# Two images side by side in a four-layer vision network: from "front and trunk" lanes to two whole-image lanes

## The chip, the cores and the metric

The kernel runs on one core of one Trainium2 chip. A core has five engines that run their own instruction queues in order: TensorE (PE, matrix multiply into PSUM), VectorE (DVE), ScalarE (ACT), GpSimd (POOL) and SyncE (SP, here used only to issue DMAs). The metric is the device time of one execution in microseconds; lower is better. All arithmetic is in float32.

## What is computed

The input is a batch of 4 images of 32x32 pixels and 384 channels. Every image passes four residual layers, each of the form `x = x + layer(group_norm(x))`. The images never meet: all reductions are within one image. Cut to what matters (one image, helper functions left out):

```python
# layer 0: deformable attention, 6 heads of 64 channels, 1024 queries and keys
q = gn(x) @ w_q + b_q
o = gelu(layernorm(grouped_conv3x3(q)))            # 6 groups
pos = tanh(o @ w_offp) * 16 + pixel_grid           # one sampling point per pixel and head
xs = bilinear_sample(gn(x), pos)                   # gathered pixels
k, v = xs @ w_k + b_k, xs @ w_v + b_v
bias = bilinear_sample(rpe, (grid - pos) * 0.5)    # [heads, 1024, 1024]
x = x + softmax(q k^T * scale + bias) v @ w_out + b_out

# layer 1: 12 heads of 32 channels, weighted by a group similarity
q, k, v = split(gn(x) @ Wqkv);  xg = gn(x) @ Wg + bg
gc = depthwise_conv3x3_stride2(xg)                 # 256 group centres
sim = sigmoid(beta + alpha * cos(xg, gc))          # [12, 1024, 256]
attn = softmax(q k^T) * (sim sim^T * gamma + 1 - gamma)
attn = attn / attn.sum(axis=query)                 # normalized over the queries
x = x + (attn v) @ Wproj

# layer 2: box sums over 5 columns and 20 channels, a quotient
# layer 3: outlook attention: 3x3 values weighted by softmax(gn(x) @ Wa), folded back
```

## The kernel before

The kernel is written against a tile framework: the Python code names tiles in pools and issues instructions, and the framework's scheduler puts the instructions of each engine in one order, places tiles in the buffers of their pools and writes the semaphores. The order in which the Python code issues work is the scheduler's priority; each engine then runs its own list strictly in that list's order.

The work on an image is cut in two parts, each written as a Python generator that yields after every small piece of work, with a number of "steps" that weighs the piece.

- **The front** (`Front.layer0`, 714 steps an image) is layer 0. `inputs0` (234 steps) loads the image, norms it, makes queries, runs the grouped convolution, computes the sampling points (`positions`), gathers pixels with indirect DMAs from the POOL queue (`gather`, line 652) and makes keys and values. Then come 12 calls of `head0` (6 heads, 2 halves of the queries, 38 steps each; with the divisions in `over_sums` 462 steps). For each of 8 blocks of 128 keys `head0` gathers a window of the bias table by an indirect DMA of POOL (line 734, tile `win`, 4 buffers), interpolates it in ACT (lines 746, 751) and DVE (747, 752), multiplies queries and keys on PE (755, into a PSUM tile `bank`), adds the two on DVE (756) and keeps a running maximum (761). Then it turns the maximum round over PE, POOL and ACT (768 to 780), and for each block subtracts it (787, DVE), takes the exponential (788, ACT) and multiplies with the values and with ones (790, PE, accumulated in one `bank` held through the 8 blocks). The output projection (18 steps) adds the residual and stores the image to DRAM.
- **The trunk** (`Trunk.image`, 1109 steps an image) is layers 1 to 3. `inputs1` (173 steps) norms, projects, runs the strided convolution and prepares softmax sums. Then come 6 calls of `pair` (two heads each, 118 steps): for each of 8 key blocks, PE makes logits (1154, into two PSUM tiles `big`), ACT exponentiates (1162), PE makes the group weights of both heads and both query halves (1184, four `bank` tiles, with transposes of kept blocks in line 1179), ACT copies parts that will be needed again (1192), DVE multiplies the weights into the exponentials (1193), and PE accumulates the values in the `bank` tile `av`, held through all 8 blocks (1128). Within the same step `sums_step` prepares the softmax sums of the next pair (1035 on PE, 1043 on DVE, 1044 on ACT, two `big` tiles). `layers23` is the tail: output projection (18 steps), layer 2 (93) and layer 3 (117).

PSUM has 8 banks: the pool `ps2` holds two tiles `big` of two banks each, the pool `ps1` four tiles `bank`. All work shares them. A pool `wts` holds three weight matrices, loaded by SP.

The main loop joins the two parts. `layer0(0)` runs the front of image 0 to its end. Then `layer3(b)` runs the trunk of image b step by step, and after each step advances the fronts of the following images until they are ahead by the trunk's share plus `LEAD` = 0.1. So trunk 0 runs with front 1, trunk 1 with front 2, trunk 2 with front 3, and trunk 3 alone. `Front` takes its tiles from the right side of SBUF, `Trunk` from the left. Front and trunk hand the image over through DRAM (`x1`).

Of the kernel before, what the change touches and what calls it, by code (L numbers as in the profile page):

```python
# [26 lines left out]
P = 128  # L27
# [24 lines left out]

R_LNG, R_LNB, R_BV0, R_BV3 = 0, C, 2 * C, 3 * C
R_BA = 4 * C
R_WOFFP = R_BA + 81
# [4 lines left out]


TRUNK_STEPS, FRONT_STEPS, LEAD = 1109.0, 714.0, 0.1

# [9 lines left out]
class Net:  # L73


    def __init__(self, ctx, tc, a):
        self.tc, self.nc, self.a = tc, tc.nc, a
        nc = self.nc
        pool = lambda name, bufs, **kw: ctx.enter_context(
            tc.tile_pool(name=name, bufs=bufs, **kw)  # L80
        )
        self.const = pool("const", 1)
        self.wts = pool("wts", 3)
        self.ps2 = pool("ps2", 2, space=PSUM)
        self.ps1 = pool("ps1", 4, space=PSUM)
        self.dram = pool("dram", 1, space=DRAM)
        self.n = 0
        self.consts()
        self.scratch()
        self.front, self.trunk = Front(self, "right"), Trunk(self, "left")  # L90

# [14 lines left out]
    def consts(self):  # L106
# [19 lines left out]
        self.rows = self.ct([P, NROW], "rows")  # L126
        nc.sync.dma_start(self.rows, a["rows"].partition_broadcast(P))
        self.blk = self.ct([P, P], "blk")
# [65 lines left out]
    def scratch(self):  # L194

        self.pairs = []
        for i in range(2):
            t = self.dram.tile([G * SLOTS, 2 * GC], F32, tag=f"pairs{i}", name=f"pairs{i}")
            self.pairs.append(t)
        dram = lambda name, shape: self.dram.tile(shape, F32, tag=name, name=name)  # L200

        self.x0 = [dram(f"x0_{i}", [C, N]) for i in range(2)]
        self.x1 = [dram(f"x1_{i}", [C, N]) for i in range(2)]

        self.qd, self.kd, self.xgd, self.yd = (dram(n, [C, N]) for n in ("qd", "kd", "xgd", "yd"))

        self.k0 = dram("k0", [C, N])
        self.gcd = dram("gcd", [C, M1])
        self.vd = dram("vd", [N, C])

        self.den = [dram(f"den{h}", [1, N]) for h in range(G)]
        self.rden = [dram(f"rden{h}", [1, N]) for h in range(G)]
        self.lse = [dram(f"lse{p}", [2, N]) for p in range(NH1 // 2)]
        self.skew = [
            self.dram.tile([NJ, P * ROWP], F32, tag=f"skew{i}", name=f"skew{i}")
            for i in range(2)
        ]
# [39 lines left out]
    def layer0(self, b):  # L257

        if b == 0:
            for _ in self.front.layer0(b):  # L260
                pass
            self.done = self.ahead = 0.0
            self.fronts = (w for i in range(1, NB) for w in self.front.layer0(i))

# [6 lines left out]
    def layer3(self, b, out):  # L271

        for w in self.trunk.image(b, out):
            self.done += w / TRUNK_STEPS
            while self.ahead < self.done + LEAD:
                self.ahead += next(self.fronts, FRONT_STEPS) / FRONT_STEPS
        assert self.ahead >= min(b + 1, NB - 1)


class Lane:  # L280


    def __init__(self, net, side):
        self.net, self.side = net, side

    def __getattr__(self, name):
# [112 lines left out]
class Front(Lane):  # L399
# [118 lines left out]
    def inputs0(self, b):  # L518
# [57 lines left out]
        for k in range(KC):  # L576
# [18 lines left out]
            yield 15  # L595
        oall = self.wt([P, NJ, C], "a12", 2)
        mv = self.wt([P, NJ, 2], "ln_mv")
        for j in range(NJ // 2):
# [24 lines left out]
        for j in range(NJ):  # L623
            v.tensor_scalar(
                oall[:, j, :],
                oall[:, j, :],
                mv[:, j, 0:1],
                rstd[:, j : j + 1],
                ALU.subtract,
                ALU.mult,  # L630
            )
            v.tensor_tensor(
                oall[:, j, :], oall[:, j, :], self.rows[:, R_LNG : R_LNG + C], ALU.mult
            )
            v.tensor_tensor(
                oall[:, j, :], oall[:, j, :], self.rows[:, R_LNB : R_LNB + C], ALU.add
            )
# [187 lines left out]
class Trunk(Lane):  # L825


    def image(self, b, out):
        with self.scope("l1y"):


            self.q4, self.k4 = self.wt([P, N], "q4"), self.wt([P, N], "k4")
            self.xg = self.wt([P, N], "xg")
# [14 lines left out]
    def inputs1(self, b):  # L848
        nc, v = self.nc, self.nc.vector
        x = self.wt([P, KC, N], "x")  # L850
        for k in range(KC):
            nc.sync.dma_start(x[:, k, :], self.x1[b % 2][k * P : (k + 1) * P, :])
        xh = self.wt([P, KC, N], "xh")
        self.norm(x, xh)
# [120 lines left out]
    def pair_tiles(self):  # L975
# [4 lines left out]
        nc = self.nc  # L980
        self.qks = [[self.wt([P, N], f"{t}{i}") for t in ("qa", "ka")] for i in range(2)]
        self.gc = self.wt([P, M1], "gc")
        for r in range(2):
            rest = slice(64 * r + HD1, 64 * r + 64)
# [6 lines left out]
    def load_sums(self, p):  # L991
# [3 lines left out]
        for h in range(2):  # L995
            rows = slice(64 * h, 64 * (h + 1))
            self.nc.sync.dma_start(self.q4[rows, :], self.qd[ch, :])
            self.nc.sync.dma_start(self.k4[rows, 0:512], self.kd[ch, h * 512 : (h + 1) * 512])

# [26 lines left out]
    def sums_step(self, i, st):  # L1026
# [4 lines left out]
        for h in range(2):  # L1031
            for r in range(2):
# [4 lines left out]
                    self.q4[rows, i * P : (i + 1) * P],  # L1037
                    self.k4[rows, 0:512],
                    start=True,
# [50 lines left out]
    def pair(self, p):  # L1090
# [6 lines left out]
        if p == 5:  # L1097

            for k, t in enumerate((self.q4, self.k4, self.xg[0:64, :])):
                nc.sync.dma_start(t, self.yd[k * P : k * P + t.shape[0], :])  # L1100
        vn = self.wt([P, NJ, 2 * HD1], "vp", 2)
        nc.sync.dma_start(
# [107 lines left out]
        values(*late.pop())  # L1210
        y = self.wt([P, 512], "y")
        nc.scalar.copy(y, av)
# [11 lines left out]
    def out1(self, b):  # L1224
# [3 lines left out]
        w = self.weights("Wproj")  # L1228
        y = (self.q4, self.k4, self.xg)
        self.mv = [self.moments() for _ in range(2)]  # L1230
# [25 lines left out]
    def layer2(self):  # L1256
        nc, v = self.nc, self.nc.vector
        with self.scope("l2"):
# [50 lines left out]

            dns = []  # L1310
            for ko in range(KC):
                ps = box20(den, ko)

                none = self.wt([P, N], "none", 2)
                v.tensor_scalar(none, ps, 0.0, None, ALU.is_equal)
                dn = self.wt([P, N], "dn", KC)
                v.scalar_tensor_tensor(dn, ps, 5.0, none, ALU.mult, ALU.add)
                x = self.x[:, ko, :]
                nc.gpsimd.tensor_tensor(x, none, x, ALU.add)
                dns.append(dn)  # L1320
            for ko in range(KC):
# [3 lines left out]
                v.tensor_tensor(x, dn, x, ALU.add)  # L1325
                self.stats(self.mv[1], self.x, ko)
                yield 14


    def layer3(self, b, out):  # L1330
        nc, v = self.nc, self.nc.vector
        skew = self.skew[b % 2]
        with self.scope("l3"):
# [97 lines left out]
            values(range(NJ // 2, NJ))  # L1431
            ys = []
            for i in range(NJ):
                pt = self.big()
                for k in range(KC):
                    nc.tensor.transpose(
                        pt[:, k * P : (k + 1) * P], self.x[:, k, i * P : (i + 1) * P], self.ident
                    )
                y = self.wt([P, C], "y", NJ)
                nc.scalar.copy(y, pt[:, 0:C])  # L1440
                ys.append(y)
            yield 20
            for i in range(NJ):
# [12 lines left out]
                v.tensor_tensor(y, ps[:, 0:C], y, ALU.add)  # L1456
                nc.sync.dma_start(out[i * P : (i + 1) * P, :], y)
                yield 4


# [82 lines left out]
```

## Time and profile before

| | us |
|---|---|
| median of 3 runs | 4879.74 |
| lowest and highest of them | 4869.65, 4883.42 |
| the profiled execution | 4916.4 |
| its span, first to last instruction | 4914.6 |
| PE busy in the span | 4251.9 (87%) |
| DVE busy | 3177.4 (65%) |
| ACT busy | 2331.1 (47%) |
| POOL busy | 934.4 (19%) |
| mean granted clock of PE | 0.905 |

The profiled execution is 0.75% longer than the median of the runs. "Busy" is the time in which an engine has an instruction under way; the granted clock is the share of its full clock that PE was given, and matmuls take longer where it is low. The times at which lines first and last appear in the trace cut the span into stages: the front of image 0 alone until about 643 us (line 432 ends it), trunk 0 with front 1 until about 1860, trunk 1 with front 2 until 3021, trunk 2 with front 3 until 4132 (line 1457 ends each), and trunk 3 alone to the end.

### The profile page before, as it was taken

To read this page: it belongs to the slowest core of one execution; us is meant where nothing else is said; L and a number is where in the kernel's file an instruction comes from. 1 tells how busy PE (TensorE), PEld (TensorE's weight loads), DVE (VectorE), ACT (ScalarE), POOL (GpSimd) and SP (SyncE) were. 2 spreads that over 40 slices of the span, in tenths; PEclk is the share of its full clock that TensorE was granted. 3 is DMA by queue.
4 is the path that set the end of the run, shared out by engine and by line. 5 is a ranking of instruction groups with operands and counts; after the bars stand their busy time and mean duration, and the time that the engine had idled before them with its cause. 6 is when DMAs were issued, how large, how long until landed. Compare 5 with 4: busy or idle time off the path is not lost.

```text
span 4914.6 us, 46753 instructions
## 1 busy us (share of the span) xinstructions
PE 4251.9 (87%) x15800; PEld 1829.4 (37%) x15800; DVE 3177.4 (65%) x5715; ACT 2331.1 (47%) x3623; POOL 934.4 (19%) x946
## 2 busy tenths in 40 slices
PE   5466677999999989889999989899999998999998
PEld 2222243333333453333333444343333335343444
DVE  3478827676878736577877763767687873455544
ACT  2155523565766213376666412356576721466630
POOL 1533203211212101331221110422121200000000
PEclk7677787999999989799999989799999998899998
DMA  5322244211212143331221123422121213201011
GB/s 116 106 81 87 69 128 143 92 55 38 76 47 74 33 145 111 104 95 49 66 58 58 55 75 111 151 88 58 32 78 44 78 34 111 91 24 30 18 38 39
DMA packets 230929, 366.84 MB, mean 75 GB/s; under 512 B 117476, under 2 KB 164673, under 8 KB 230689
## 3 DMA queue, kind: packets, MB, share of 16 engines
q1 hardware_dynamic: 169672, 197.36, 13.5%
q0 software_dynamic: 39936, 145.53, 9.7%
q10 hardware_dynamic: 21080, 20.96, 1.7%
q8 instruction: 125, 2.05, 0.2%
q14 instruction: 116, 0.94, 0.1%
HBM read 285.84 MB, written 78.21 MB: 74 GB/s over the span
## 4 chain that ended last, share of the span: by engine, by line
PE 50%; DVE 11%; ACT 11%; issue 5%; DMA 2%; POOL 1%; another core or an unknown queue 0%; SPq 0%; ACTq 0%; DVEq 0%; POOLq 0%
PE bank L1184 10%; PE big L376 5%; PE big L1154 5%; PE big L1035 4%; PE bank L755 4%; PE bank L790 4%; PE bank L390 3%; PE bank L1128 3%; ACT big L1044 3%; PE bank L1179 2%; PE big L1284 2%; DVE e L1193 2%; DVE nmax L1043 2%; ACT e L1162 1%; PE big L584 1%
## 5 line engine op out<-in xcount | busy, mean ns | idle before, releaser
L1193 DVE SCALAR_TENSOR_TENSOR e<-bank,gam,e 128x512 f32<-128x512 f32 x768 | 558.2, 749 | 568.3 <-ACT gn L1192 274.5
L1184 PE MATMUL bank<-sim,sg 128*128 128x512 f32 (+3 forms) x2304 | 879.6, 516 | 6.2 <-POOL sg L1139 3.7
L1044 ACT ACTIVATE big<-big,nmax 128x1024 f32<-128x1024 f32 x384 | 418.5, 1090 | 392.2 <-DVE nmax L1043 340.4
L734 POOL DMA_INDIRECT win<-strips,widx x384 | 421.2, 1097 | 876.6 <-DVE z L747 450.7
L1184 PEld LDWEIGHTS bank<-sim,sg 128*128 128x128 f32 x2304 | 408.7, 200 | 386.2 <-issue 303.6
L1162 ACT ACTIVATE e<-big 128x1024 f32<-128x1024 f32 x384 | 376.7, 1019 | 359.9 <-PE big L1154 354.7
L1043 DVE TENSOR_REDUCE nmax<-big 128x1 f32<-128x1024 f32 x384 | 453.7, 1219 | 74.4 <-PE big L1035 46.5
L1035 PE MATMUL big<-k,q 32*128 32x512 f32 x1536 | 353.6, 691 | 86.6 <-ACT e L1162 36.6
L1154 PE MATMUL big<-qa,ka 64*128 64x512 f32 x1536 | 412.9, 629 | 14.8 <-ACT big L1044 8.9
L1139 POOL TENSOR_SCALAR sg<-sim,gam 128x512 f32<-128x512 f32 x192 | 148.2, 774 | 1429.3 <-PE bank L1184 1135.5
L790 PE MATMUL bank<-lg,va 128*64 128x512 f32 x768 | 373.6, 635 | 39.8 <-ACT lg L788 39.7
L755 PE MATMUL bank<-qpad,kz 128*128 128x512 f32 x768 | 378.2, 622 | 21.4 <-DVE e L1193 13.2
L790 PE MATMUL bank<-lg,ones 128*64 128x512 f32 x768 | 372.9, 635 | 0.0
L746 ACT ACTIVATE z<-win,bias_f 128x528 f32<-128x528 f32 x384 | 277.2, 738 | 181.5 <-DVE lg L752 105.3
L752 DVE SCALAR_TENSOR_TENSOR lg<-z,bias_f,lg 128x512 f32<-128x512 f32 x384 | 300.8, 798 | 45.5 <-ACT lg L751 43.7
L747 DVE SCALAR_TENSOR_TENSOR z<-win,bias_f,z 128x528 f32<-128x528 f32 x384 | 292.0, 781 | 36.0 <-DMA win<-strips,widx 24.3
L652 POOL DMA_INDIRECT gat<-pairs,sidx x192 | 206.2, 1074 | 485.6 <-DVE ix_gt L464 241.6
L756 DVE TENSOR_TENSOR lg<-bank,lg 128x512 f32<-128x512 f32 x384 | 256.9, 685 | 60.3 <-PE bank L755 58.7
L787 DVE TENSOR_TENSOR lg<-lg,tb 128x512 f32<-128x512 f32 x384 | 250.6, 711 | 61.3 <-ACT tb L780 61.3
L751 ACT ACTIVATE lg<-z,bias_f 128x512 f32<-128x512 f32 x384 | 268.0, 719 | 44.3 <-DVE z L747 27.4
L788 ACT ACTIVATE lg<-lg 128x512 f32<-128x512 f32 x384 | 223.2, 630 | 85.4 <-DVE lg L787 85.1
L1154 PEld LDWEIGHTS big<-qa,ka 64*128 64x128 f32 x1536 | 135.8, 189 | 272.2 <-issue 157.0
(253 smaller groups left out, 5844.8 us busy)
## 6 DMA issues: line engine op xcount, KB each, us to landing
pairs<-xn SPq DMA_DIRECT2D x64, 192.0 KB
q<-qd SPq DMA_DIRECT2D x48, 256.0 KB
w<-in_gmat SPq DMA_DIRECT2D x16, 576.0 KB
w<-in_w_off SPq DMA_DIRECT2D x12, 576.0 KB
w<-in_Wqkv SPq DMA_DIRECT2D x12, 576.0 KB
a<-in_x SPq DMA_DIRECT2D x16, 384.0 KB
x<-a ACTq DMA_DIRECT2D x4, 1536.0 KB
k<-a SPq DMA_DIRECT2D x12, 512.0 KB
```

The source lines that it names most:

```text
L734: nc.gpsimd.indirect_dma_start(out=win, out_offset=None, in_=self.strips[:, :], in_offset=bass.IndirectOffsetOnAxis(ap=self.widx[:, q, c : ...
L747: v.scalar_tensor_tensor(z, wv[:, 1 : HH + 1, 0 : HW + 1], sc(0, 1), z, ALU.mult, ALU.add)
L752: v.scalar_tensor_tensor(lg, z[:, :, 1 : HW + 1], sc(0, 0), lg, ALU.mult, ALU.add)
L755: nc.tensor.matmul(ps, kz[:, j * P : (j + 1) * P], both, start=True, stop=True)
L790: nc.tensor.matmul(po[out, :], w, lf, start=j == 0, stop=j == NJ - 1)
L1035: nc.tensor.matmul(ps[r][:, h * 512 : (h + 1) * 512], self.q4[rows, i * P : (i + 1) * P], self.k4[rows, 0:512], start=True, stop=True,)
L1043: v.tensor_reduce(nmax[:, r, i : i + 1], ps[r], AX.X, ALU.max, negate=True)
L1044: nc.scalar.activation(ps[r], ps[r], AF.Exp, bias=nmax[:, r, i : i + 1], accum_out=den[:, r, i : i + 1],)
L1154: nc.tensor.matmul(ps[:, r, :], ka[rows, j * P : (j + 1) * P], qa[rows, cols], start=True, stop=True,)
L1162: nc.scalar.activation(e, ps, AF.Exp)
L1184: nc.tensor.matmul(ps[:, (mid - i0) * P :], sg[:, r, m, :], sim[:, r, m, mid * P : i1 * P], start=m == 0, stop=m == 1,)
L1193: v.scalar_tensor_tensor(e[:, r, :], ps, self.gam[:, 1:2], e[:, r, :], ALU.add, ALU.mult, accum_out=tot[:, r, h : h + 1],)
```

## The change

`Front` and `Trunk` become base classes of one class `Image`, and there are two objects of it, the lanes. Lane 0 runs images 0 and 2, lane 1 images 1 and 3, each through all four layers: `layer0`, then `image`. Lane 0 has its tiles on the left side of SBUF, lane 1 on the right. The main loop collects the outputs' addresses and, at the last image, advances whichever lane has done less, counted in steps (1823 an image); lane 1 counts from `LAG` = 0.07 of an image, that is 128 steps behind lane 0. Each lane gets DRAM scratch of its own.

So that a whole image fits in half of SBUF, tiles are cut: the layer norm's gain and offset are loaded for each image into a tile `ln_gb` instead of being kept with the constants; `inputs1` norms in place (`xh = x`); `k4` is half as long; `q4` and `k4` live only in layer 1, and the first buffers of `qa` and `ka` hold the output of layer 1 instead; `none` has one buffer for two; `dn` two for three, so that the third denominator of layer 2 is made after the first quotient; the turned rows `y` of layer 3 have 4 buffers for 8, made four ahead; the pair's output `y` shares the buffers of `vp`. The pool `wts` has 4 buffers for 3.

The arithmetic is the same. In the two built programs PE has 8946 instructions, DVE 4949 and POOL 951 on both sides (loading of registers and waits not counted), and SP issues 4 DMAs more, those of `ln_gb`.

```diff
-TRUNK_STEPS, FRONT_STEPS, LEAD = 1109.0, 714.0, 0.1
+STEPS, LAG = 1823.0, 0.07
...
-        self.wts = pool("wts", 3)
+        self.wts = pool("wts", 4)
...
-        self.front, self.trunk = Front(self, "right"), Trunk(self, "left")
+        self.lanes = [Image(self, i, side) for i, side in enumerate(("left", "right"))]
+        self.outs = []
...
     def layer0(self, b):
-        if b == 0:
-            for _ in self.front.layer0(b):
-                pass
-            self.done = self.ahead = 0.0
-            self.fronts = (w for i in range(1, NB) for w in self.front.layer0(i))
+        pass
...
     def layer3(self, b, out):
-        for w in self.trunk.image(b, out):
-            self.done += w / TRUNK_STEPS
-            while self.ahead < self.done + LEAD:
-                self.ahead += next(self.fronts, FRONT_STEPS) / FRONT_STEPS
-        assert self.ahead >= min(b + 1, NB - 1)
+        self.outs.append(out)
+        if b < NB - 1:
+            return
+        lanes = [lane.images(range(i, NB, 2)) for i, lane in enumerate(self.lanes)]
+        done = [0.0, LAG]
+        while min(done) < NB:
+            i = done.index(min(done))
+            step = next(lanes[i], None)
+            done[i] = NB if step is None else done[i] + step / STEPS
...
+        ln = self.wt([P, 2, C], "ln_gb")
+        nc.sync.dma_start(
+            ln.rearrange("p t c -> p (t c)"), self.a["rows"][0 : 2 * C].partition_broadcast(P)
+        )
...
-            self.q4, self.k4 = self.wt([P, N], "q4"), self.wt([P, N], "k4")
+            self.qks = [tuple(self.wt([P, N], t) for t in ("qa0", "ka0"))]
...
-        xh = self.wt([P, KC, N], "xh")
+        xh = x
...
-                none = self.wt([P, N], "none", 2)
+                none = self.wt([P, N], "none")
...
-                dn = self.wt([P, N], "dn", KC)
+                dn = self.wt([P, N], "dn", 2)
...
+            dns = [denominator(0), denominator(1)]
             for ko in range(KC):
...
+                if ko + 2 < KC:
+                    dns.append(denominator(ko + 2))
...
-                y = self.wt([P, C], "y", NJ)
+                y = self.wt([P, C], "y", 4)
...
+                if i + 4 < NJ:
+                    ys.append(turned(i + 4))
...
+class Image(Front, Trunk):
+    def images(self, which):
+        for b in which:
+            yield from self.layer0(b)
+            yield from self.image(b, self.outs[b])
```

## The prediction

> **What bounds the kernel now.** I read the busy slices first: they show where one engine is full and where none is.
>
> ```profile
> PE   5466677999999989889999989899999998999998
> DVE  3478827676878736577877763767687873455544
> ACT  2155523565766213376666412356576721466630
> ```
>
> In the first five slices (the front of image 0 alone) DVE is the fullest engine at 7 or 8 tenths and PE stands at 4 to 7; from there on PE is at 9. In the last seven slices (trunk 3 alone) PE is at 9 and DVE at 4 or 5. Next the stages: front 0 alone, three trunks with the next front, trunk 3 alone. Columns are start and end, length, then busy us and count of PE, PEld (weight loads), DVE, ACT and POOL, the granted PE clock, DMA share and GB/s.
>
> ```profile
> 0.00:643.00 643.00, 365.95 (x1144) 144.49 (x1144) 407.42 (x643) 235.10 (x382) 197.00 (x196) 0.75 0.34 93
> 643.00:1860.00 1217.00, 1103.83 (x4222) 481.74 (x4226) 799.09 (x1444) 594.82 (x930) 226.23 (x219) 0.92 0.27 82
> 1860.00:3021.00 1161.00, 1055.98 (x3954) 451.96 (x3950) 791.19 (x1426) 582.85 (x907) 230.75 (x232) 0.93 0.26 78
> 3021.00:4132.00 1111.00, 1014.85 (x3682) 429.55 (x3674) 783.83 (x1409) 569.90 (x884) 228.08 (x230) 0.93 0.24 74
> 4132.00:4914.60 782.60, 711.27 (x2806) 321.64 (x2806) 395.84 (x794) 348.48 (x521) 52.33 (x71) 0.94 0.14 43
> ```
>
> The two ends, 643 + 783 = 1426 us or 29% of the span, run one image alone: no engine is over 63% busy in the first, and DVE is half idle in the last. A front and a trunk together take 1163 us on average. Last the two ends piece by piece, because the changed kernel is made of the same pieces in other company: the front's inputs (two rows), its heads and its output; then the trunk's `inputs1` (two rows), its pairs, its output with layer 2, and layer 3.
>
> ```profile
> 0.00:106.00 106.00, 62.65 (x352) 32.39 (x352) 31.30 (x70) 25.75 (x47) 16.92 (x39) 0.82 0.68 134
> 106.00:222.00 116.00, 44.06 (x109) 22.42 (x110) 52.86 (x82) 4.11 (x9) 51.53 (x48) 0.63 0.25 78
> 222.00:620.00 398.00, 244.52 (x656) 83.54 (x654) 317.85 (x487) 205.25 (x326) 127.37 (x108) 0.76 0.27 83
> 620.00:643.00 23.00, 14.72 (x28) 6.14 (x28) 5.41 (x6) 0.00 (x0) 1.18 (x1) 0.78 0.49 155
> 4132.00:4192.00 60.00, 51.67 (x134) 24.57 (x134) 30.46 (x50) 12.07 (x15) 8.15 (x16) 0.86 0.30 99
> 4192.00:4267.00 75.00, 65.43 (x173) 25.83 (x171) 25.97 (x25) 31.69 (x50) 1.36 (x2) 0.75 0.36 118
> 4267.00:4753.00 486.00, 460.02 (x2073) 196.82 (x2072) 258.89 (x607) 288.44 (x433) 31.69 (x46) 1.00 0.09 23
> 4753.00:4849.00 96.00, 77.60 (x199) 35.43 (x198) 59.47 (x62) 8.58 (x9) 7.46 (x5) 0.90 0.09 29
> 4849.00:4914.00 65.00, 56.55 (x238) 39.00 (x238) 21.04 (x53) 7.69 (x15) 3.66 (x2) 0.83 0.24 73
> ```
>
> The heads alone hold DVE 317.85 of 398 us (80%); the pairs alone hold PE 460.02 of 486 us (94.7%) at full clock. The waits of those two stretches, longest first (what DVE waits for in the heads, what PE waits for in the pairs):
>
> ```profile
> DVE dens L808 <- DMA dens<-den: 19.1, 2, 9.9
> DVE lg L787 <- ACT tb L780: 14.1, 6, 4.3
> DVE lg L756 <- PE bank L755: 12.8, 17, 2.3
> ```
>
> ```profile
> PE big L1074 <- ACT sim L1081: 8.9, 5, 1.8
> PE bank L1179 <- DVE e L1193: 8.4, 5, 1.7
> PE big L1035 <- ACT big L1044: 4.1, 5, 0.8
> ```
>
> All are waits for the lane's own previous step, which another image would fill.
>
> **The change part by part.** No work is taken away: the instruction counts are equal. What moves is which pieces run beside each other. Lane 1 is 128 steps behind lane 0, so like runs with like: heads with heads, pairs with pairs. I walk through the stages, lane 0 / lane 1, in steps; a piece's time for part of its steps is taken in proportion.
>
> A: lane 0's first 128 steps (most of the inputs) with little beside them. Alone they take 106 us (first row). In the built program's SP order lane 1's image load already stands behind lane 0's convolution weights, so lane 1 starts within that: 60 to 106, taken as 95.
> B1: lane 0's last 106 input steps / lane 1's first 128. Alone 116 and 106; DVE sums to 53 + 31 = 84, PE to 107, so neither is full and the chains' own length decides: 116 to 222 (no overlap), taken as 130, nearer the longer chain since the engines have room.
> B2: lane 0's first 106 of 462 head steps / lane 1's last inputs. DVE 317.85 x 106/462 = 73, and 53: 126 at least, 207 at most (91 + 116); taken at 94% of DVE, 135.
> B3: heads / heads, 356 steps each. DVE 2 x 317.85 x 356/462 = 490. PE 377 (at the low clock of that row), ACT 316, POOL 196 lie under it. DVE's share decides: 98% gives 500, the single lane's 80% gives 612. I take 94%, what the fullest engine reaches in the pairs alone, because DVE's waits above (its 80 idle us) are for one lane's DMA, maximum and matmul, and in the built order the other lane's operations stand between: 520.
> C: lane 1's last 106 head steps and output / lane 0's first 128 of `inputs1`. DVE 73 + 5 + 42 = 120, PE 56 + 15 + 87 = 158 at clocks of 0.75 to 0.86 (at full clock some 130): 120 to 214, taken as 150.
> D: trunk / trunk, without lane 0's first and lane 1's last 128 steps. PE is full. Two trunks have 2 x 711 = 1422 busy; less 87 (in C) and 65 (in E: all of layer 3 and a little of layer 2), 1270. Of this 920 are pairs at full clock; 350 ran at about 0.84, and with pairs beside them would run near 1.00: 294. So 1214 at full clock. At the pairs' own share of 94.7% that is 1282, at 98% 1239; if the cold pieces stay cold, 1270/0.947 = 1341. PE's order in the built program alternates one whole pair step of each lane, the same string of matmuls as in the trunk alone, with looser dependences. I take 1290.
> E: lane 1's last 128 steps / lane 0's next image, first 128. Alone 73 and 106; PE 65 + 63 = 128: 106 to 179, taken as 140.
> I: lane 1's last 128 steps alone: 73, taken as 80.
>
> B to D come twice: 95 + 2 x (130 + 135 + 520 + 150 + 1290) + 140 + 80 = 95 + 4450 + 220 = 4765, against 4914.6. Medians stand at 4879.74/4916.4 = 0.9926 of that: 4730.
>
> The small edits. `ln_gb`'s 4 loads go on SP ahead of the image's stores, and land long before line 632 reads them; the one-buffer `none`, the two `dn` and in-place norm lengthen a lane's layer 2 and `inputs1` chains by a few DVE operations' wait (about 1 us each in these rows), covered by the other lane's matmuls; uncovered, in I, about 5 us. With 4 buffers, a copy of `y` waits in ACT's queue for an output store, and behind it the other lane's ACT work; ACT is at most 59% busy in every row of the trunk, so this costs nothing while it has room, and at worst 16 copies x 9.9 us (the longest DMA wait shown above) = 158 if each waited in full. Weights: 4 buffers, but lane 0's next ones are loaded early and hold them through its pairs; lane 1's first load then waits on SP until lane 0 leaves, which it does 128 steps earlier. POOL: clearing a lane's next tiles waits there for the lane's last store, ahead of the other lane's gathers; those have 4 windows in hand. These I leave in the 94%.
>
> The granted clock is 0.76 in the heads alone against 1.00 in the pairs. The Trainium skill, "TensorE: Matmul & The Clock Gate", section "HAM oscillation — how this bites in real kernels", says that idle gaps of more than about 3.4 us halve PE's clock again, which speaks against joining two stages in which DVE is the bound. By that rule B3 and C would stay at half clock for much of the time; PE's 377 us in B3 already are at the low clock and still lie under DVE's 490, so the sum would change only in C, by some 20 us a time.
>
> **The rivals.** (1) PSUM. Each lane's pair holds one `bank` (`av`) through its 8 blocks, so two of four are left for the group weights, where the trunk alone has three. PE fills one with two matmuls of up to 634 ns (line 1184), then ACT's copy (up to 584 ns, line 1192) and DVE's product (749 ns, line 1193) follow before it is free. For it: DVE waits 174 + 274 us for line 1192's copies over the span. Against it: between two fills of a pair stand a `sums_step` (4 matmuls of 691 ns, line 1035) or the next logits (4 of 629 ns, line 1154). D gains until PE's share there falls to 1214/1365 = 89% (75 us more in each of two D, all that separates 4765 from 4915); at 86% D is 1412, the whole 5009, the median 4972: slower.
> (2) Heads in phase do not fill each other: one in-order POOL and DVE queue for both lanes makes one wait for the other. At the single lane's 80% B3 is 612, the whole 4949, the median 4912, a little slower; the turn is at 82%. For it: a gather in POOL's order often stands ahead of the other lane's line 774. Against it: POOL is 32% busy in the heads.
> (3) Everything fills: A 70, B1 120, B2 128, B3 500, C 135, D 1239, E 125, I 73: 4512, median 4480. For it: the other lane covers every wait shown above. Against it: mixed stages reach no more than 91% of PE today.
> (4) The lanes drift out of step, so that fronts meet trunks as today: about 4880. Against it: the alternating order in the built program.
>
> **How the numbers follow.** Forecast 0.55 with 4600 to 4860 as its own range; (1) 0.17; (2) 0.12; (3) 0.13; (4) 0.03. A measurement here tells 0.3% from no change (the runs spread by 0.28%), 4865 to 4894. Faster: 0.55 + 0.13 and a little of (2), 0.70. Slower: (1) and half of (2), 0.22. Same: 0.08. The range takes in the forecast, most of (2), the near half of (1) and of (3): 4540 to 4930.
>
> **What would show it.** Right: DVE at 9 tenths for about 500 us twice, once from about 360 us and once from about 2720; PE at 9 for 1300 us from about 1030 and again to the end; a short tail of 80 us. Wrong: PE in the pairs waiting for DVE's line 1193 or ACT's copies before the group weights (rival 1); DVE near 80% in the heads with waits of `win` or `tb` (rival 2); stages of trunk with front in one window (rival 4). If PE's share in D is under 89%, or DVE's in B3 under 82%, the forecast falls.

## The result and the profile after

| | before | after |
|---|---|---|
| median (lowest to highest), us | 4881.58 (4869.65 to 4886.24), 4 runs | 5219.94 (5211.7 to 5223.59), 4 runs |
| span of the profiled execution | 4914.6 | 5219.9 |
| PE busy in the span | 4251.9 | 4308.0 |
| PE idle in the span (span less busy) | 662.7 | 911.9 |

The changed kernel is slower: ratio 1.0695, 95% interval 1.0671 to 1.0718. That is 338 us more by the medians, and 490 more than the 4730 predicted. The two spans differ by 305: 56 more in PE's busy time, 249 more in its idle time.

The totals and the slices of the changed kernel (40 slices of 130 us, busy tenths) show where the idle time went:

```profile
span 5219.9 us, 46486 instructions
...
PE 4308.0 (83%) x15800; PEld 1818.4 (35%) x15800; DVE 3175.9 (61%) x5715; ACT 2365.0 (45%) x3614; POOL 981.2 (19%) x946
...
PE   6627667799999999999886376677999999999998
...
DVE  3478988764454555456444688887544555564464
```

The tail with one lane alone is down to about 60 us. But twice, in slices 3 to 8 and 23 to 28, PE stands at 6 or 7 tenths and at the beginning at 2 or 3, while DVE is at 6 to 9. These are the two meetings of two fronts. In between PE is at 9 and DVE mostly at 4 or 5: two trunks. The kernel before had stretches with two lanes in which PE was at 9 and DVE at 7 at the same time.

The stages of the first round (columns as in the prediction: start and end, length, busy us and counts of PE, PEld, DVE, ACT, POOL, granted clock, DMA share, GB/s). The first row is B2, the second B3, the third C, the other four together D. B2 begins with lane 0's first heads (line 751, at 248.2 us), B3 with the end of lane 1's inputs (line 716, at 447.6), C with lane 0's first store of its output (line 433, at 1004.6):

```profile
248.00:448.00 200.00, 93.21 (x280) 40.36 (x272) 147.79 (x248) 71.89 (x114) 101.05 (x83) 0.73 0.34 102
448.00:1003.00 555.00, 384.22 (x1012) 121.13 (x1013) 486.69 (x747) 318.93 (x499) 196.93 (x164) 0.79 0.32 92
1003.00:1190.00 187.00, 161.45 (x444) 66.57 (x441) 116.50 (x174) 69.31 (x106) 26.37 (x33) 0.89 0.33 111
1190.00:1440.00 250.00, 230.50 (x758) 97.24 (x756) 116.38 (x194) 118.18 (x175) 17.05 (x28) 0.90 0.28 88
1440.00:2283.00 843.00, 805.30 (x3521) 338.64 (x3520) 446.87 (x1033) 494.39 (x744) 54.34 (x80) 0.98 0.10 25
2283.00:2460.00 177.00, 170.67 (x603) 80.68 (x602) 99.77 (x176) 47.32 (x58) 17.03 (x15) 0.96 0.09 27
2460.00:2566.00 106.00, 93.31 (x285) 45.51 (x283) 64.57 (x79) 12.39 (x19) 10.49 (x5) 0.91 0.24 75
```

The stages are the ones foreseen, in the order foreseen; each of these is longer than its term. In the heads (second row) DVE is busy 487 of 555 us and PE 384. In D PE is busy 1300 of 1376 us. In B2 no engine is above 74%: that stage is waiting.

What the heads wait for (448 to 1003 us; us in total, times, longest):

```profile
POOL win L738 <- DVE z L751: 205.1, 36, 15.7
...
DVE lg L760 <- PE bank L759: 49.5, 42, 3.7
...
PE bank L794 <- ACT lg L792: 44.9, 20, 3.7
```

The lines are those of before moved by 4: 738 is the window gather (734), 751 the interpolation (747), 759 the queries times keys (755), 760 the sum (756), 792 the exponential (788), 794 the product with the values (790). POOL's wait is harmless while windows are in hand. Of DVE's 68 idle us, 49.5 are behind line 759. The other two rows make a ring: DVE waits for one lane's 759, which stands in PE's queue behind the other lane's 794, and for 794 PE itself has often waited on an exponential of ACT just before. (While DVE waits, PE is busy with 759 and 794 for all but 0.3 us; 32 of the 42 waits fall in a run of PE's work that began with such a wait.) With one lane the trace showed 12.8 us of DVE's wait in 398 us of heads; with two it is 49.5 in 555. How much of B3's excess the ring makes is not shown.

B2 as POOL sees it, 285 to 335 us (start, duration, engine, line, operation, tiles; in brackets the idle time ahead and what ended it):

```profile
293.31 3.35 POOL L738 DMA_INDIRECT win<-strips,widx  x1 [32.04 <-DVE z L751]
...
308.62 1.15 POOL L656 DMA_INDIRECT gat<-pairs,sidx  x1 [0.35 <-DVE sidx L494]
...
331.96 0.95 POOL L656 DMA_INDIRECT gat<-pairs,sidx  x1 [0.30 <-issue]
333.21 0.94 POOL L738 DMA_INDIRECT win<-strips,widx  x1 [0.30 <-issue]
```

A window gather of lane 0's heads first waits 32 us for its buffer, which DVE's line 751 has to free. In that time DVE is mostly at lane 1's layer norm and sampling points (some of its rows):

```profile
273.33 0.86 DVE L628 TENSOR_SCALAR a<-a,ln_mv,ln_rstd 128x384 f32<-128x384 f32 x2
...
283.00 1.01 DVE L639 TENSOR_TENSOR a<-a,ln_gb 128x384 f32<-128x384 f32 x2
...
284.67 3.36 DVE L445 TENSOR_TENSOR a<-a,rows 128x3072 f32<-128x3072 f32 x1
...
291.81 0.76 DVE L751 SCALAR_TENSOR_TENSOR z<-win,bias_f,z 128x528 f32<-128x528 f32 x1
```

Lines 628 to 639 stand in its list as one block, from 273 to 284 us; then come sweeps of lines 445 and 446 of 3.35 us, with single steps of the heads between them. When lane 1 has its indices, its pixel gathers (line 656), 18 of them in a row, hold POOL from 308.62 to 333.21 us, and no window is fetched. So the heads of one lane and the inputs of the other take turns at DVE and POOL instead of filling each other.

### The profile page after: what moved, and what is told of

The parts are those of the page before. It is cut to its first block, busy times and chain, and to the rows that moved or that the text cites. A ratio compares the mean times of both kernels' runs of the same rounds, so it can differ in the third digit from the quotient of the medians.

```text
span 5219.9 us, 46486 instructions
## 1 busy us (share of the span) xinstructions
PE 4308.0 (83%) x15800; PEld 1818.4 (35%) x15800; DVE 3175.9 (61%) x5715; ACT 2365.0 (45%) x3614; POOL 981.2 (19%) x946
## 4 chain that ended last, share of the span: by engine, by line
PE 56%; DVE 15%; ACT 8%; issue 7%; DMA 3%; POOL 3%; SPq 0%; ACTq 0%; DVEq 0%; POOLq 0%
PE bank L1190 13%; PE big L1160 6%; PE bank L794 6%; PE big L1041 4%; PE big L376 4%; PE bank L1134 3%; PE bank L390 3%; PE bank L759 3%; PE bank L1185 3%; DVE lg L760 3%; ACT big L1050 2%; POOL gat L656 2%; PE big L1290 2%; DVE z L751 2%; DVE nmax L1049 2%
## 5 line engine op out<-in xcount | busy, mean ns | idle before, releaser
L1190 PE MATMUL bank<-sim,sg 128*128 128x512 f32 (+3 forms) x2304 | 847.0, 501 | 0.3 <-DVE e L1199 0.3
L738 POOL DMA_INDIRECT win<-strips,widx x384 | 465.8, 1213 | 1023.2 <-DVE z L751 540.8
L1145 POOL TENSOR_SCALAR sg<-sim,gam 128x512 f32<-128x512 f32 x192 | 133.6, 699 | 2149.3 <-PE bank L1190 1400.6
L1190 PEld LDWEIGHTS bank<-sim,sg 128*128 128x128 f32 x2304 | 396.2, 195 | 358.6 <-issue 287.6
L794 PE MATMUL bank<-lg,va 128*64 128x512 f32 x768 | 419.5, 688 | 95.2 <-ACT lg L792 95.2
L759 PE MATMUL bank<-qpad,kz 128*128 128x512 f32 x768 | 435.4, 691 | 12.0 <-DVE lg L760 11.8
L794 PE MATMUL bank<-lg,ones 128*64 128x512 f32 x768 | 417.7, 686 | 0.0
L1041 PE MATMUL big<-k,q 32*128 32x512 f32 x1536 | 306.3, 655 | 41.6 <-ACT big L1050 22.3
L656 POOL DMA_INDIRECT gat<-pairs,sidx x192 | 220.3, 1148 | 193.3 <-DVE ix_gt L464 124.9
L794 PEld LDWEIGHTS bank<-lg,va 128*64 128x64 f32 x768 | 107.4, 156 | 414.4 <-ACT lg L792 244.1
```

Of the source, the lines that this page charges most:

```text
L738: nc.gpsimd.indirect_dma_start(out=win, out_offset=None, in_=self.strips[:, :], in_offset=bass.IndirectOffsetOnAxis(ap=self.widx[:, q, c : ...
L759: nc.tensor.matmul(ps, kz[:, j * P : (j + 1) * P], both, start=True, stop=True)
L794: nc.tensor.matmul(po[out, :], w, lf, start=j == 0, stop=j == NJ - 1)
L1041: nc.tensor.matmul(ps[r][:, h * 512 : (h + 1) * 512], self.q4[rows, i * P : (i + 1) * P], self.k4[rows, :], start=True, stop=True,)
L1190: nc.tensor.matmul(ps[:, (mid - i0) * P :], sg[:, r, m, :], sim[:, r, m, mid * P : i1 * P], start=m == 0, stop=m == 1,)
```

## The experiments

Two theories at the start. P (pairing): what costs is that like meets like, whichever lanes do it. Q: what costs is what whole-image lanes bring with them, the cut tiles, the shared queues and the two halves of SBUF. For each kernel its edit stands against the kernel named. Each ratio is to the kernel before on the same chip.

### The cut tiles alone

The kernel before, with its front and trunk lanes, and the small edits of the change (each lane's own DRAM scratch too), but for the fourth buffer of weights.

```diff
+        ln = self.wt([P, 2, C], "ln_gb")
...
-        xh = self.wt([P, KC, N], "xh")
+        xh = x
...
-                none = self.wt([P, N], "none", 2)
+                none = self.wt([P, N], "none")
...
-                dn = self.wt([P, N], "dn", KC)
+                dn = self.wt([P, N], "dn", 2)
...
-                y = self.wt([P, C], "y", NJ)
+                y = self.wt([P, C], "y", 4)
```

> The kernel before, with its front and trunk lanes, its order and its 3 weight buffers, but with all the tile cuts of the change (ln_gb loaded per image, norm in place, short k4, one none, two dn, four y, shared vp). P: the cuts cost nothing that matters, within 1% of the kernel before (4830 to 4930). Q: they carry the loss, 5050 or more.

Measured: 4889.39 us (10 runs), ratio 1.0008 (0.9996 to 1.0019). The cuts cost 4 us at the most likely and 9 at the interval's end. They are out.

### The distance between the lanes

The changed kernel with another `LAG`, nothing else.

```diff
-STEPS, LAG = 1823.0, 0.07
+STEPS, LAG = 1823.0, 0.39
```

> The changed kernel with LAG 0.39 (711 steps) for 0.07, so that a lane's front always runs beside the other lane's trunk; nothing else differs. Theory P (the loss is the company: two fronts are bound by DVE while PE idles, two trunks by PE while DVE idles): stages summed with the rates measured in the changed kernel, 643 + 888 + 532 + 867 + 888 + 532 + 495 = 4845 in the profile, median 4700 to 4950, that is at least 270 below 5220. Theory Q (the loss is the smaller tiles, the shared queues and the PSUM of two whole-image lanes, whatever their lag): the median stays above 5100.

> LAG 0.25 (456 steps). P: the second half of a front's heads meets the other lane's inputs, its trunk's beginning meets the other's heads: 413 + 310 + 570 + 888 + 562 + 310 + 570 + 888 + 317 = 4828, median 4700 to 4950. Q: above 5100, no trend with the lag.

> LAG 0.5 (911 steps): a front meets only pairs of the other lane, at the price of longer ends alone. P: 794 + 863 + 261 + 863 + 250 + 863 + 261 + 633 = 4788, median 4650 to 4950. Q: above 5100.

> The changed kernel with LAG 0: both lanes in step. P: all like pieces meet, nothing is gained on 0.07 but some 110 us of lane 0 alone at the start and 60 of lane 1 at the end are filled, and maxima and exponentials of both heads now fall together: 5150 to 5300.

| LAG | median us | ratio (95%) |
|---|---|---|
| 0 (2 runs) | 5366.18 | 1.0995 (1.0965 to 1.1026) |
| 0.07 (the change) | 5219.94 | 1.0695 (1.0671 to 1.0718) |
| 0.25 | 5109.27 | 1.0462 (1.0436 to 1.0487) |
| 0.39 | 5076.8 | 1.0396 (1.0371 to 1.042) |
| 0.5 | 5086.09 | 1.0415 (1.0393 to 1.0436) |

The nearer the lanes are in phase, the slower, up to 0.39: P has the direction, and Q, which expected no trend, has not. But none of the four medians lies in P's range: three are 127 us or more above it, and with `LAG` 0 the kernel is 66 slower than the range allowed. At 0.39, where a front should lie beside a trunk, only 143 of the 338 us come back, where P's sums asked for nearly all. The trace says why (`LAG` 0.39, a stretch with lane 0 in its trunk and lane 1 in its heads, then a stretch with both in their trunks):

```profile
1003.00:1600.00 597.00, 544.70 (x2013) 204.66 (x2011) 460.12 (x853) 386.08 (x603) 123.39 (x119) 0.95 0.21 61
1600.00:2139.00 539.00, 507.61 (x1888) 224.99 (x1889) 275.83 (x523) 217.44 (x317) 40.18 (x51) 0.96 0.20 60
```

Both lanes advance by equal counts of steps, and a front is 714 of 1823, a trunk 1109. So whatever the lag, some 400 steps or more of each round have two trunks side by side: in the second row PE is full at 94% and DVE at 51%, and the DVE work that is not done there has to be done elsewhere. The steps' ratio is the kernel's own weight, not a time, and with the lag alone the change can't be turned back.

### The pace as well

`LAG` 0.5, and a front's steps weighted so that a front takes as much of the count as a trunk, as the kernel before has it.

```diff
-STEPS, LAG = 1823.0, 0.07
+STEPS, LAG = 2218.0, 0.5
...
-            yield from self.layer0(b)
+            for w in self.layer0(b):
+                yield w * 1109 / 714
```

> Two whole-image lanes with the company and the pace of the kernel before: every step of a front counts 1109/714 (an image 2218), LAG 0.5, so that one lane's whole front is spread over the other lane's whole trunk. LAG 0.39 and 0.5 at equal pace won back only some 140 of the 340 us. Theory P' (what is left is pace: there a front is used up within 714 of the trunk's 1109 steps, and the rest pairs trunk with trunk): median 4850 to 4950, as the kernel before. Theory Q' (whole-image lanes cost about 190 us in themselves, by their queues or the hand-over within a lane): 5030 to 5100.

Measured: 5010.26 us, ratio 1.0277 (1.026 to 1.0294): 67 us below the best lag alone (58 by the ratios), and between the two expectations. Every round is now front beside trunk, in whole-image lanes, and 129 us are still missing against the kernel before.

### POOL's gathers

The changed kernel with the window gathers left out: all windows are one tile of zeros, made once for each image.

```diff
+                self.still = self.wt([P, (HW // 2 + 1) * WROW], "win")
+                nc.gpsimd.memset(self.still, 0.0)
...
-            win = self.wt([P, (HH + 1) * WROW], "win", 4)
-            nc.gpsimd.indirect_dma_start(
...
-            )
+            win = self.still
```

> The changed kernel (LAG 0.07) without the 384 window gathers of POOL: head0 reads one still window of zeros per image, which leaves out the position bias; all of DVE's, ACT's and PE's work stays. Theory W (with two fronts in phase a lane's windows stand in POOL's queue behind the other lane's pixel gathers): the stretch in which lane 0's first heads meet lane 1's inputs falls from 200 to about 150 us and the heads in phase from 555 to about 520, twice: 5030 to 5080. Theory D (DVE's own work and order set these stretches): 5180 or more.

Measured: 5147.81 us (2 runs), ratio 1.0553 (1.0532 to 1.0574): 72 us less, between the two expectations. B2 and B3 between the same events as in the change (lane 0's first heads, the end of lane 1's inputs, lane 0's first store):

```profile
247.00:428.00 181.00, 94.73 (x280) 41.97 (x272) 143.62 (x242) 65.46 (x108) 58.32 (x51) 0.74 0.18 55
428.00:973.00 545.00, 378.43 (x1010) 120.46 (x1012) 484.78 (x745) 320.21 (x497) 25.93 (x19) 0.80 0.04 12
```

B2 takes 181 us for 200, B3 545 for 555. POOL falls from 197 to 26 us in B3, and DVE stays at 485 us, now 89% of the stage. So the gathers are a part of the loss (36 us a round, 29 of them in B2 and B3, which together lie 100 over their terms), most of it in B2, and they are not what holds the heads. The run takes out POOL's instructions and the transfers that they start; it doesn't separate the two.

### Less work for DVE

In the kernel before and in the changed one, the running maximum of a head is taken over blocks 0, 1 and 7 alone. 5 of 7 maxima in each of 48 head calls, 240 instructions of 0.68 us, are left out: 163 us of DVE.

```diff
-            elif j > 1:
+            elif j == NJ - 1:
```

> The changed kernel with 240 of its 336 DVE maxima in the heads left out (the running maximum takes blocks 0, 1 and 7 alone), 240 x 681 ns = 163 us less on DVE and nothing else. P (DVE is the bound while two fronts run together): 120 to 160 us faster, 5060 to 5100. Rival (waits across the lanes, not DVE's work, set the heads): under 60 us faster, above 5160.

> The same 163 us of DVE work left out of the kernel before. P (three of its four fronts lie under PE's trunk work): only the front alone gains, 30 to 40 us, and the others at most 15 each: 4800 to 4855. If DVE bounds its mixed stages too, 120 us or more: under 4765.

Measured: changed kernel 5087.64 us, ratio 1.0437 (1.0418 to 1.0455), 132 less than with all maxima; kernel before 4836.98, ratio 0.9906 (0.9881 to 0.9931), 45 less. One and the same 163 us of DVE work is worth 81% of itself in the changed kernel and 27% in the kernel before, and both totals lie where P expected them. Of the 45 us, 27 belong to the one front that runs alone: its last sum (line 432) in the kernel before, then in the one with fewer maxima:

```profile
641.80 1.28 DVE L432 SCALAR_TENSOR_TENSOR res<-big,cols,res 128x1024 f32<-128x1024 f32 x1 [3.89 <-PE big L376]
```

```profile
615.27 1.28 DVE L432 SCALAR_TENSOR_TENSOR res<-big,cols,res 128x1024 f32<-128x1024 f32 x1 [3.89 <-PE big L376]
```

That leaves some 18 of 122 us for the three fronts beside trunks. (By the two traces it would be 53; but the one of the kernel before is 35 us above its median.) In the changed kernel the fronts' end shows the gain directly. The last store of layer 0, which ends the second meeting of two fronts, moves from 3783.8 to 3634.3 us, 150 of the 163 us:

```profile
L433 SPq DMA_DIRECT2D x<-res x12: 319/320/431, 1004.6 to 3783.8; - x12
```

```profile
L433 SPq DMA_DIRECT2D x<-res x12: 319/320/432, 934.5 to 3634.3; - x12
```

DVE sets the pace of paired fronts, and much less that of the old mixed stages. (The second kernel is the only one here that is faster than the kernel before; it does less work.)

### The lead, in the kernel before

In the kernel before, the next front runs 0.1 ahead of the trunk that it accompanies; the paced lanes have no such lead. Theory H: the 129 us left are the missing lead, not the lanes.

```diff
-TRUNK_STEPS, FRONT_STEPS, LEAD = 1109.0, 714.0, 0.1
+TRUNK_STEPS, FRONT_STEPS, LEAD = 1109.0, 714.0, 0.001
```

> The kernel before, LEAD 0.001 for 0.1: a front ends with the trunk beside it, as in the paced lanes, where an image's trunk must follow its own front at once. The paced lanes came to 5010 against 4882. Theory H (that rest is the missing lead: the output of a front, the start of its trunk, the other image's tail and the next inputs, all short chains, fall together): 4960 to 5030. Theory L (the rest lies in the lanes themselves, their halves of SBUF and scratch): within 30 us of the kernel before.

> The kernel before with LEAD 0.2 for 0.1. H: the lead helps further only if chains still meet at 0.1: 4840 to 4890. If a larger lead takes company from the pairs, 4900 to 4950.

Measured: without lead 5050.66 us, ratio 1.0352 (1.0331 to 1.0373); with 0.2, 4991.33, ratio 1.0229 (1.021 to 1.0248), above the expectation too. More lead is no help either: 0.1 lies between two slower settings. The old lanes without lead are 40 us slower than the paced whole-image lanes. Between the two traces, 135 us apart, all of the loss lies in the three mixed stages: 3624 us in place of 3489, with ends of 641 + 784 in place of 643 + 783. Where two stages change over, around 1700 us, the kernel without lead and the paced lanes look alike. First without lead, then paced, then the kernel before:

```profile
1700.00:1750.00 50.00, 31.57 (x88) 16.29 (x87) 46.68 (x50) 6.24 (x9) 11.33 (x6) 0.76 0.10 30
```

```profile
1700.00:1750.00 50.00, 27.37 (x88) 14.05 (x86) 45.39 (x64) 17.13 (x27) 12.04 (x8) 0.66 0.16 49
```

```profile
1700.00:1750.00 50.00, 42.94 (x112) 19.55 (x113) 36.57 (x35) 6.11 (x9) 10.98 (x7) 0.84 0.28 96
```

Without lead and paced, DVE is full (47 and 45 of 50 us) and PE at 32 and 27: layer 2 of the trunk, whose quotients are on DVE (three reciprocals of line 1323 take 19.6 us of the first row), meets the front's last heads. In the kernel before the same 50 us have PE at 42.94 and DVE at 36.57. This is one stretch of 50 us; what makes up the whole 135 us was not added up.

### The lead, in whole-image lanes

The paced lanes with lane 1 started 0.05 of a round earlier.

```diff
-STEPS, LAG = 2218.0, 0.5
+STEPS, LAG = 2218.0, 0.45
```

> The paced lanes of the run before (5010 us), with lane 1 started 0.05 of a round earlier, which is 0.1 of a front: lane 1's fronts (images 1 and 3) now lead lane 0's trunks by 0.1 as in the kernel before, while lane 0's second front (image 2) starts 0.1 of a front behind lane 1's trunk. In the kernel before, taking the lead from all three mixed stages cost 172 us, 57 each. Theory H (what is left of the loss at equal pace is the missing lead): two stages win about 57 each, the one that now lags loses something up to 57: 4890 to 4960, below 5000 in any case. Rival K (lanes cannot lead each other in turn; what one stage wins the next pays): 4990 to 5030, with image 2's front later by what image 1's was earlier. Rival M (the lead does nothing in whole-image lanes; the two losses are equal by chance): 5000 to 5020 and no stage changed by over 20 us.

Measured: 4932.92 us (10 runs) beside 4909.04 for the kernel before on that chip (13 runs), ratio 1.0051 (1.0033 to 1.0069). H's total holds. Its place doesn't, and there rival M, which expected no stage to change by over 20 us, was right: the mixed stages took 1195, 1181 and 1166 us (3542) where the paced lanes had 1188, 1195 and 1182 (3565), 23 us less, and none changed by more than 16. The greater part is at the ends. Start and end of the paced lanes, then of this kernel:

```profile
0.00:648.00 648.00, 361.38 (x1144) 143.10 (x1144) 411.64 (x643) 233.69 (x381) 192.98 (x181) 0.75 0.36 96
...
4213.00:4999.00 786.00, 710.92 (x2806) 321.03 (x2806) 396.20 (x795) 348.89 (x521) 50.67 (x70) 0.94 0.14 43
```

```profile
0.00:681.00 681.00, 405.98 (x1420) 166.07 (x1424) 419.13 (x660) 249.02 (x407) 198.62 (x182) 0.78 0.38 101
...
4223.00:4918.00 695.00, 632.37 (x2597) 284.76 (x2595) 356.19 (x736) 325.90 (x488) 44.24 (x55) 0.94 0.12 33
```

276 of front 1's matmuls now run inside the first front's idle time, and the last trunk starts earlier beside the one before it: 1434 us of ends become 1376, 58 of the 81 us between the two spans.

## Why the prediction was wrong

The sum's terms against the trace (us; the second round from the stages at the same points, B1 from 2715 to D's end at 5160):

| term | predicted | round 1 | round 2 |
|---|---|---|---|
| A | 95 | 106 | |
| B1 inputs / inputs | 130 | 142 | 125 |
| B2 heads / inputs | 135 | 200 | 201 |
| B3 heads / heads | 520 | 555 | 553 |
| C heads / `inputs1` | 150 | 187 | 189 |
| D trunk / trunk | 1290 | 1376 | 1377 |
| E | 140 | 149 | |
| I | 80 | | 59 |

Against 4765 the span is 455 too long: 173 from D, 131 from B2, 76 from C, 68 from B3, and 7 from the rest. Two steps failed: the busy time of PE in D, and the overlap taken for B2, B3 and C. (One reading of the slices is rounded: in the first two DVE stands at 3 and 4, not at 7 or 8. The sum rests on the stage rows, which are read rightly.)

**What bounds each stage** was right: DVE in the heads, PE in the trunks. DVE's 490 us in B3 came as 487, PE's 158 in C as 161.

**D, the step that failed in size.** PE's share there was taken as 94.1% (1214 of 1290) and is 94.5%. What failed is the busy time: "350 ran at about 0.84, and with pairs beside them would run near 1.00: 294". PE is busy for 1300 us in D, not 1214, and that is 30 more than even the 1270 without any gain. The granted clock over D is 0.96, where trunk 3 alone has 0.94; in D's first and last row it is 0.90 and 0.91. The cold pieces stayed cold for the greater part.

A mean clock also doesn't say which matmuls had it. The projections of line 376 stand among the pieces counted at 0.84. Here they are alone in trunk 3 (4132 to 4267 us, mean clock 0.80) and then in D (1190 to 1440, mean clock 0.90), mean ns behind the busy time:

```profile
L376 PE MATMUL big<-xh,w 128*128 128x512 f32 x108 | 49.5, 617 | 1.4 <-DVE xh L357 1.4
```

```profile
L376 PE MATMUL big<-x,w 128*128 128x512 f32 x108 | 50.6, 623 | 3.6 <-ACT big L1050 3.4 <-ACT sim L1087 0.2
```

In trunk 3 all 108 of them ran between 4147 and 4207 us, and there the clock was nearly full; the low clock lies in the 60 us behind them:

```profile
4147.00:4207.00 60.00, 60.00 (x144) 24.69 (x144) 27.75 (x37) 15.63 (x20) 0.00 (x0) 0.97 0.32 106
4207.00:4267.00 60.00, 50.43 (x134) 19.30 (x133) 22.65 (x22) 26.71 (x43) 1.36 (x2) 0.69 0.35 113
```

So these 50 us had next to nothing to gain from company, though the mean clock of their window is 0.80. A stage's busy time can't be multiplied by the ratio of two mean clocks. Over all forms, a matmul takes 711.27 us / 2806 = 253 ns on average in trunk 3 and 1300 / 5167 = 252 in D; the mixes are not quite the same. The prediction's own alternative, "if the cold pieces stay cold, 1341", was the better one. The 35 us above it are for the most part those 30 us of busy time, whose cause is not shown. The Trainium skill, "Perfetto Trace Analysis", section "Tensor Engine Instruction (MATMUL, LD_WEIGHTS)", says that a matmul's end in the trace is computed from the instruction's size and not observed, so that a mean like 617 ns is partly a model. No run here separates model and matmul; the length of D is measured.

**B2, B3 and C, the step that failed in overlap: "I take 94%".** The fullest engine's share from the pairs alone was carried to stages in which work passes between several engines. B3 reached 88%, B2 74% of DVE, C 86% of PE. B2's 200 us are nearly the 207 that the prediction gave for no overlap at all. "POOL is 32% busy in the heads" was the argument against a shared queue; it is 35% in B3 and 51% in B2, and its share says nothing of the 32 us for which it waits for a buffer. The price of the turn by turn in B2, 66 us a round, was in no rival: rival 2 names the shared queues and prices B3 alone. Windows without gathers win back 29 of the 100 us that B2 and B3 lose in a round, most of it in B2. That the rest lies in DVE's order and in the ring of 759, 760, 792 and 794 is argued from the waits; no run took it apart.

**Rival 1 (PSUM banks)** is refuted. A pair step with another pair beside it takes 10.38 us; alone, 10.53. In each of the groups below a step has four of these products (289 in the 750 us from 1500 in the changed kernel, 152 in the 400 us from 4300 before):

```profile
L1199 DVE SCALAR_TENSOR_TENSOR e<-bank,gam,e 128x512 f32<-128x512 f32 x289 | 210.5, 749 | 323.1 <-ACT gn L1198 169.8 <-ACT gf L1198 81.9 <-PE bank L1185 39.8
```

```profile
L1193 DVE SCALAR_TENSOR_TENSOR e<-bank,gam,e 128x512 f32<-128x512 f32 x152 | 110.0, 749 | 171.7 <-ACT gn L1192 102.8 <-ACT gf L1192 39.8 <-PE bank L1179 14.6
```

The sign named for this rival, PE waiting for DVE's product before it can fill a bank, got smaller: 1.7 us in these 750 us, where the trunk alone had 8.4 in 486.

```profile
L1185 PE MATMUL bank<-ident,gn 128*128 128x128 f32 x216 | 45.7, 295 | 1.9 <-DVE e L1199 1.7
```

Nor is there much of a gain: PE was full alone, and a twin beside it wins 1.4%.

**Rival 2 (heads don't fill each other)** is about half right: DVE's share went from the single lane's 80% to 88%, not to 94%. Its sign was half right too: DVE waits little for `tb` there, and mostly for line 759.

**Rival 3** (everything fills) asked for 98% of DVE in B3, where the trace has 88%; **rival 4** (the lanes drift) didn't happen: both rounds have the same stages within 2 us from B2 on. **Small edits**: at nothing, as taken (ratio 1.0008; the fourth buffer of weights had no run of its own). **The clock gate**: the granted clock in B3 is 0.79 though PE is 69% busy, and in C it is 0.89. As foreseen the low clock of B3 lies under DVE's time. The rule of the Trainium skill, "TensorE: Matmul & The Clock Gate", section "HAM oscillation — how this bites in real kernels", agrees with this in direction where two stages bound by DVE are joined. That C would stay at half clock for much of the time doesn't fit its 0.89, and no run here tests the 3.4 us.

**What the working left out.** The sign could have been had from the rows shown. Paired with its like, a front costs DVE's 407.42 us and a trunk PE's 711.27. Less the pieces in A and E (31 and 65), a round is 2 x 407.42 + 2 x 711.27 - 96 = 2141, if nothing of a front hides behind a trunk. The forecast's round, 2225, had these engines busy for 96% of it, over five stages. The mixed stages of the kernel before, with one front and one trunk, have PE at 91%. As an estimate, at 91% the round is 2353, the whole 95 + 2 x 2353 + 140 + 80 = 5021: slower. The chip gave 87 and 88%.

**Where the 338 us are.** In ratios: from 1.0695 the company of the lanes (`LAG` 0.39) takes 0.030, the pace 0.012, the lead 0.023; 0.005 is left. The first two are one cause, like beside like. The third was tried as the same cause, and in the kernel before it does lie in the mixed stages, while in whole-image lanes it works mostly at the ends; why is not shown. What whole-image lanes bring with them, the cut tiles, the fourth buffer, the halves of SBUF, costs 0.005 on balance once all three are undone. On balance, because the ends of the paced lanes with lead are 50 us shorter than those of the kernel before, and their mixed stages, 3542 us for 3489, are 53 longer. Why they are longer stays open, and so does, as said, how B2 and B3 share their loss among DVE's order and the ring.

## What to carry to other kernels

Pair stages whose fullest engines differ. For any pairing, add up the fullest engine's busy time stage by stage and divide by the share that two-lane stages of the same kernel already reach; a stage that has one engine full alone gains next to nothing from a twin (1.4% here), and a forecast that asks for a better share than any stage shows should say why. Where two lanes share in-order queues, the distance, the pace and the lead between them were worth 143, 67 and over 100 us here, and the lead in both directions (`LEAD` 0.001, 0.1, 0.2: 5051, 4878, 4991 us), so they are to be measured and not argued.

## What the runs showed of the hardware

- A DVE saving's worth depends on the company: 163 us of work were worth 132 us where fronts meet fronts. In the kernel before they were worth 45, of which 27 belong to the front that runs alone.
- The mean granted clock of a window is not the clock of the matmuls in it: from 4132 to 4267 us the mean was 0.80, but the 108 projections took 617 ns each, on average, in a part of it that had 0.97, and the 60 us behind them had 0.69.
- Two lanes of heads on one DVE and POOL get 88% out of DVE where one gets 80%; with 171 us of POOL's work taken out of a 555 us stage, the stage is 10 us shorter and DVE's share 89%.
